# A sampling table with one column of two rows per entry, read two entries at a time

## The chip, the core and the metric

The kernel runs on one core of a Trainium2 chip. The core has a matrix engine (PE), a vector engine (DVE), a scalar engine (ACT), a general engine (POOL), a queue engine that only issues transfers (SP), and 16 DMA engines that all queues share. The metric is the time on the device in microseconds, as the median of several runs. Beside the timed runs there is one execution under the hardware profiler; its trace and its page of sums are what this document quotes.

## What is computed

The reference takes a batch of eight images of 64 channels and 128 x 128 pixels through four layers. The first is a deformable convolution, and only this layer is touched. For every pixel and each of the nine taps of a 3 x 3 kernel, two small convolutions give an offset and a mask; the image is sampled at the shifted place by bilinear interpolation, which needs four neighbouring pixels:

```
def corner(yi, xi, wgt):
    valid = (yi >= 0) & (yi < H) & (xi >= 0) & (xi < W)
    ...
    return vals * (wgt * valid)[None]
return corner(y0, x0, wy0 * wx0) + corner(y0, x0 + 1, wy0 * wx1) + corner(y0 + 1, x0, wy1 * wx0) + corner(y0 + 1, x0 + 1, wy1 * wx1)
...
sampled = sampled * mask[:, None]
return jnp.einsum('bckhw,ock->bohw', sampled, weight.reshape(O, C, KK))
```

The other layers are a 3 x 3 convolution, a bidirectional state-space scan over rows and columns, and a search for the nine least similar pixels of a window, followed by a convolution. Everything is in 32-bit floats. In the kernel the image is normalised before the deformable layer, in groups of two channels.

## The kernel before

The images are handled in four pairs. Two images of 64 channels fill the 128 partitions.

**The stages of the first layer.** `deform` (from L176) holds four generators. `statistics(p)` loads a pair in eight pieces and gathers mean and variance. `fill(p)` (L272 to L302) writes a sampling table in HBM for each of the two images. `offsets(p, e)` computes the offsets of eight image rows: it loads the rows into `xe` (L310), normalises them on ACT, and runs the offset convolutions as a long chain of matmuls (L322) for each group of four rows; results are transposed back (`to`) and `positions` (from L341) turns them into table indices `idx` and four weights per sample `wts` on DVE. `sample(p, g, ...)` (from L376) does the sampling proper for four image rows.

**The table.** One entry of the table stands for one pixel place and holds four pixels of 64 channels: the place itself, the one below, the one to the right, and that one's lower neighbour. That is 256 floats, or 1,024 bytes. The table has `CELL` = 131 rows and 131 columns of such entries, with borders of zeros for places outside the image. The zeros are written once, before anything else, by DMAs from ACT's queue (L201, L203, L204). Two pairs of tables are used in turn.

**The fill.** It runs in 33 steps. A step takes four image rows: PE transposes them (L289), so that a partition is a column of the image; DVE and ACT copy them into a tile `q` (L291 to L293) as two-row columns, where each column holds a pixel and the one below it, 128 floats. Then four DMAs go out on SP's queue: for each of the two images, the same `q` is written once into the left half of entries (L299) and once, one column further left, into the right half (L300). Image pieces `xt` of 16 rows are loaded on the same queue (L285), into two buffers; `q` has three buffers.

**The gather.** For every partition (one image column), image row and tap, one entry is fetched. POOL issues one indirect DMA for 128 samples (L388); nine of them fill a tile `g`, of which there are four. DVE multiplies a gathered entry by its four weights (L397) and adds the four products (L398) into `sm`; PE transposes `sm` (L402, L404), ACT copies it (L405, L406), and at the end of four rows PE applies the weights of the deformable convolution (L411). There are 4 pairs x 32 groups x 72 gathers = 9,216 gathers.

**The order.** The first table and the first offsets are made before any sampling: `run(statistics(0))`, `run(fill(0))`, `run(offsets(0, 0))`. After that the sampling loop advances the next offsets after every ninth gather, and the statistics and the fill of the next pair after every third of these. A scheduler lays out the instructions of each engine ahead of time, and the engines keep to that order. An indirect DMA waits for all writes to its table; so the first gather comes after the whole first fill.

Of the kernel before, what the change touches and what calls it, by code (L numbers as in the profile page):

```python
# [9 lines left out]
F32 = mybir.dt.float32  # L10
I32 = mybir.dt.int32
AF = mybir.ActivationFunctionType
ALU = mybir.AluOpType
# [3 lines left out]
P = 128  # L17
C = 64
H = 128
# [2 lines left out]
NCH = HW // CH  # L22
ROOM = 2 * (H // 2 + 1) * H
CELL = H + 3
QW = 4 * C
NS = 64
T = 4
NB = 256
# [12 lines left out]
class Net:  # L41
# [134 lines left out]
    def deform(self):  # L176
        tc, nc, ins = self.tc, self.nc, self.ins
# [5 lines left out]
        with ExitStack() as ctx:  # L183
# [6 lines left out]
            bias = cp.tile([54, 1], F32, name="bias")  # L190


            tables = [[self.dram.tile([CELL, CELL, QW], F32, name=f"table{s}{i}") for i in range(2)] for s in range(min(2, self.npair))]
            with tc.tile_pool(name="a_setup", bufs=1) as sp:
                zeros = sp.tile([P, 6 * C], F32, name="zeros")
                nc.gpsimd.memset(zeros, 0.0)
                for table in (t for pair in tables for t in pair):
                    flat = table.rearrange("a b q -> a (b q)")
                    n = CELL * QW // P
                    for row in (0, CELL - 1):  # L200
                        nc.scalar.dma_start(flat[row : row + 1, :].rearrange("a (p n) -> (a p) n", p=P), zeros[:, 0:n])  # L201
                    for r0, r1 in ((1, CELL - 1 - 1), (CELL - 2, CELL - 1)):
                        nc.scalar.dma_start(flat[r0:r1, 0 : 6 * C], zeros[0 : r1 - r0, :])  # L203
                        nc.scalar.dma_start(flat[r0:r1, CELL * QW - 6 * C :], zeros[0 : r1 - r0, :])  # L204
                whv = sp.tile([P, 2, 15, 2, 9], F32, name="whv")
                wmm = sp.tile([P, 9, 9], F32, name="wmm")
                for i in range(2):
                    rows = slice(i * C, (i + 1) * C)
                    nc.sync.dma_start(whv[rows, 0], ins["wh"])
                    nc.sync.dma_start(whv[rows, 1], ins["wv"])  # L210
                    nc.sync.dma_start(wmm[rows], ins["wm"])
                for i in range(2):
                    rows = slice(i * C, (i + 1) * C)
                    for d in range(-7, 8):
                        if d:
                            nc.vector.tensor_copy(wt[rows, at[0, d], 0:2, i, :], whv[rows, 0, d + 7])
                            nc.gpsimd.tensor_copy(wt[rows, at[d, 0], 0:2, i, :], whv[rows, 1, d + 7])
                    nc.vector.tensor_add(wt[rows, 0, 0:2, i, :], whv[rows, 0, 7], whv[rows, 1, 7])
                    for a in range(3):
                        for b in range(3):  # L220
                            nc.vector.tensor_copy(wt[rows, at[a - 1, b - 1], 2, i, :], wmm[rows, 3 * a + b])
                bh = sp.tile([36, 2], F32, name="bh")
                for d in range(2):
                    for i in range(2):
                        to = slice(18 * d + 9 * i, 18 * d + 9 * i + 9)
                        for n, b in enumerate(("bh", "bv")):
                            nc.sync.dma_start(bh[to, n : n + 1], ins[b][d].rearrange("(k o) -> k o", o=1))
                nc.vector.tensor_add(bias[0:36, :], bh[:, 0:1], bh[:, 1:2])
                for i in range(2):
                    nc.sync.dma_start(bias[36 + 9 * i : 45 + 9 * i, :], ins["bm"].rearrange("(k o) -> k o", o=1))  # L230
# [41 lines left out]
            def fill(p):  # L272

                r, nb = norms[p]
                table = tables[p % len(tables)]

                q = qp.tile([P, 2, 4, 2, C], F32, tag="q", name=f"q{p}_0")
                nc.gpsimd.memset(q[:, :, 0, 0, :], 0.0)
                for g in range(NCH + 1):
                    n = 4 if g < NCH else 1  # L280
                    if g < NCH:
                        if g % 4 == 0:
                            xs = xp.tile([P, 16, H], F32, tag="xs", name=f"xt{p}_{g}")
                            xf = xs.rearrange("p h w -> p (h w)")
                            nc.sync.dma_start(xf, self.x[p * P : (p + 1) * P, g * CH : (g + 4) * CH])  # L285
                            nc.scalar.activation(xf, xf, AF.Identity, bias=nb, scale=r)
                        tp = ps_t.tile([P, 4, 2, C], F32, tag="tp", name=f"tp{p}_{g}")
                        for m in range(4):
                            nc.tensor.transpose(tp[:, m].rearrange("p i c -> p (i c)"), xs[:, 4 * (g % 4) + m, :], self.ident)  # L289
                        nxt = qp.tile([P, 2, 4, 2, C], F32, tag="q", name=f"q{p}_{g + 1}")  # L290
                        nc.vector.tensor_copy(q[:, :, :, 1, :].rearrange("p i r c -> p r i c"), tp)  # L291
                        nc.scalar.copy(q[:, :, 1:4, 0, :].rearrange("p i r c -> p r i c"), tp[:, 0:3])
                        nc.vector.tensor_copy(nxt[:, :, 0, 0, :], tp[:, 3])  # L293
                    else:
                        nc.gpsimd.memset(q[:, :, 0, 1, :], 0.0)
                    for i in range(2):
                        rows = table[i][4 * g + 1 : 4 * g + 1 + n]
                        src = q[:, i, 0:n].rearrange("p r t c -> p r (t c)")
                        nc.sync.dma_start(rows[:, 2 : 2 + H, 0 : 2 * C].rearrange("r w e -> w r e"), src)  # L299
                        nc.sync.dma_start(rows[:, 1 : 1 + H, 2 * C :].rearrange("r w e -> w r e"), src)  # L300
                    q = nxt
                    yield  # L302

            def offsets(p, e):
# [8 lines left out]
                for g in (2 * e, 2 * e + 1):  # L313
# [22 lines left out]
                    nc.vector.tensor_copy(off[:, :, 4 * (g % 2) : 4 * (g % 2) + 4, :].rearrange("p d r n -> p r d n"), tp)  # L336
                    yield
                ready[p, e] = positions(p, e, off)
                yield

            def positions(p, e, off):  # L341

                n = 8 * 18
                h0 = 8 * e
                pos = op.tile([P, 2, n], F32, tag="pos", name=f"pos{p}_{e}")
                cell = op.tile([P, 2, n], F32, tag="cell", name=f"cell{p}_{e}")
                up = op.tile([P, 2, n], F32, tag="up", name=f"up{p}_{e}")
                o = off.rearrange("p d r n -> p d (r n)")
                nc.vector.scalar_tensor_tensor(pos[:, 0], base_y, float(h0), o[:, 0], ALU.add, ALU.add)
                nc.vector.tensor_add(pos[:, 1], base_x, o[:, 1])  # L350

                nc.vector.tensor_scalar(pos, pos, -2.0, float(H), ALU.max, ALU.min)
                whole = up.bitcast(I32)
                nc.vector.tensor_copy(whole, pos)
                nc.vector.tensor_copy(cell, whole)
                nc.vector.tensor_tensor(up, cell, pos, ALU.is_gt)
                nc.vector.tensor_sub(cell, cell, up)

                nc.vector.tensor_sub(pos, pos, cell)
                nc.vector.tensor_scalar(up, pos, -1.0, 1.0, ALU.mult, ALU.add)  # L360
                idx = wp.tile([P, n], I32, tag="idx", name=f"idx{p}_{e}")
                nc.vector.scalar_tensor_tensor(cell[:, 0], cell[:, 0], float(CELL), cell[:, 1], ALU.mult, ALU.add)
                nc.vector.tensor_scalar_add(idx, cell[:, 0], float(2 * CELL + 2))
                mask = o[:, 2]
                nc.scalar.activation(mask, mask, AF.Sigmoid)
                nc.vector.tensor_mul(pos[:, 0], pos[:, 0], mask)
                nc.vector.tensor_mul(up[:, 0], up[:, 0], mask)
                w = wtp.tile([P, n, 2, 2], F32, tag="wts", name=f"wts{p}_{e}")
                for b, wx in ((0, up), (1, pos)):
                    for a, wy in ((0, up), (1, pos)):  # L370
                        nc.vector.tensor_mul(w[:, :, b, a], wx[:, 1], wy[:, 0])
                w = w.rearrange("p n b a -> p n (b a)")
                wts = [w[:, 0 : n // 2], w[:, n // 2 :]]
                return idx, wts
# [47 lines left out]

            run(statistics(0))
            run(fill(0))
            run(offsets(0, 0))
            for p in range(self.npair):
# [4 lines left out]
                for e in range(NCH // 2):  # L431
# [12 lines left out]
                    idx, wts = ready.pop((p, e))  # L444
# [933 lines left out]
```

## Time and profile before

| what | us |
|---|---|
| median of three timed runs | 16,778.65 |
| lowest and highest of them | 16,744.45 and 16,786.79 |
| the profiled execution | 18,868.66 |
| its span, first to last instruction | 18,866.9 |
| first table write issued, first gather | 81.7 and 233.1 |
| last gather | 14,066.5 |

The profiled execution took some 12% longer than the timed runs, so sums made from its rows stand against its own time. A row of the page's fifth part reads: line, engine, operation, what is written and read, how many; then busy time in total and the mean of one in ns; then the engine's idle time just before and what ended it. A line of a stage gives start and end, the length, busy time and count for PE, PE's weight loads, DVE, ACT and POOL, the granted clock of PE as a share, the mean busy share of the 16 DMA engines and GB/s. Issuing a DMA is not counted as busy time, except on POOL[...].

The transfers of the page, in packets, megabytes and share of the engines' time:

```profile
q0 software_dynamic: 442368, 1208.55, 21.9%
q1 hardware_dynamic: 519524, 751.65, 13.1%
```

The first is the queue of the gathers (9,216 x 128 x 1,024 bytes), the second SP's queue, with the table writes among its traffic.

### The profile page before, as it was taken

The numbers are of one execution on the slowest core, as the hardware profiler recorded it, in microseconds if no ns is written. First come the engines' busy times: TensorE is split into PE (matmuls) and PEld (weight loads), VectorE is DVE, ScalarE is ACT, GpSimd is POOL, SyncE is SP. The second block draws the span as 40 slices with busy tenths as digits, with TensorE's granted clock in tenths as the row PEclk, the third lists the DMA queues.
The fourth block names the chain that finished last, engine by engine and source line by source line (L and its number), as shares of the span: only waits on it lengthen the run. The fifth ranks groups of instructions, "written<-read, shape, count | busy, mean of one in ns | idle before, by whom it ended". The sixth has DMA issues, their size and how long they took to land. (4 is left out here: it accounts for less than half of the span.)

```text
span 18866.9 us, 120155 instructions
## 1 busy us (share of the span) xinstructions
PE 11118.0 (59%) x31864; PEld 4087.3 (22%) x31864; DVE 11443.6 (61%) x27208; ACT 2993.5 (16%) x5596; POOL 11190.9 (59%) x10484
## 2 busy tenths in 40 slices
PE   4654445545555444545544554455328988888886
PEld 1111111111111111111111111111104444444443
DVE  4565666665665556656656565556564755657566
ACT  1000010010100000111000000000013424334242
POOL 3676777677666677676767767667762414324142
PEclk7776776767777666777777776667659989989898
DMA  5333344334433333444333333333332242432423
GB/s 177 97 102 97 120 132 124 115 123 125 127 118 97 95 98 112 122 129 125 101 92 98 97 96 100 95 95 98 90 119 63 65 143 77 118 91 75 133 75 97
DMA packets 1036955, 2006.36 MB, mean 106 GB/s; under 512 B 204140, under 2 KB 572148, under 8 KB 1012724
## 3 DMA queue, kind: packets, MB, share of 16 engines
q0 software_dynamic: 442368, 1208.55, 21.9%
q1 hardware_dynamic: 519524, 751.65, 13.1%
q10 hardware_dynamic: 74384, 38.46, 0.9%
q8 instruction: 260, 4.26, 0.1%
q14 instruction: 419, 3.43, 0.1%
HBM read 1544.92 MB, written 276.80 MB: 97 GB/s over the span
## 5 line engine op out<-in xcount | busy, mean ns | idle before, releaser
L388 POOL DMA_INDIRECT g<-table,idx x9216 | 9704.6, 1053 | 4132.2 <-issue 2620.7
L398 DVE TENSOR_REDUCE sm<-g 128x64 f32<-128x256 f32 x9216 | 5039.8, 580 | 2991.7 <-remote 2020.0
L322 PE MATMUL po<-xe,wt 128*54 128x512 f32 (+3 forms) x8384 | 4637.8, 663 | 295.7 <-ACT ob L332 177.5
L402 PE MATMUL sp<-ident,sm 128*128 128x128 f32 x4096 | 1499.5, 376 | 4621.1 <-DVE sm L398 2058.2
L397 DVE TENSOR_TENSOR g<-g,wts 128x256 f32<-128x256 f32 x9216 | 3538.2, 415 | 663.8 <-DMA g<-table,idx 577.6
L402 PEld LDWEIGHTS sp<-ident,sm 128*128 128x128 f32 x4096 | 620.7, 155 | 7332.1 <-DVE sm L398 2490.0
L405 ACT COPY s<-sp 128x512 f32<-128x512 f32 x1024 | 598.9, 585 | 9839.8 <-PE sp L402 4174.9
L411 PE MATMUL yp<-s,wd 128*64 128x512 f32 (+1 forms) x2560 | 875.3, 700 | 925.6 <-ACT s L405 560.9
L322 PEld LDWEIGHTS po<-xe,wt 128*54 128x54 f32 x8384 | 913.8, 138 | 1618.9 <-issue 1156.8
L412 DVE BATCH_NORM_STATS2 ystat<-yp 128x6 f32<-128x512 f32 x128 | 89.2, 697 | 1318.5 <-remote 838.5
L839 POOL COPY l_yb<-ln_y 128x512 f32<-128x512 f32 x128 | 79.0, 658 | 1309.6 <-PE l1v L833 1166.7
L562 PE MATMUL c<-room,l_w 128*64 128x508 f32 (+1 forms) x3072 | 741.6, 597 | 21.7 <-DMA room<-nx 15.5
L1205 POOL TENSOR_TENSOR u<-u,v 128x512 f32<-128x512 f32 x256 | 330.9, 1292 | 696.0 <-DVE v L1204 515.2
L1297 POOL TENSOR_TENSOR ms<-ms,ln_y 128x512 f32<-128x512 f32 x256 | 278.3, 1107 | 743.6 <-DVE ln_y L118 711.5
L404 PE MATMUL s<-ident,sm 128*64 128x128 f32 x1024 | 344.6, 337 | 628.4 <-DVE sm L398 267.1
L1187 ACT ACTIVATE fx<-room,ln_b,ln_g 128x512 f32<-128x512 f32 x512 | 639.4, 1294 | 118.7 <-DMA in<-fx 99.6
L1220 DVE TENSOR_TENSOR_SCAN z<-tabs,z,u 128x256 f32<-128x256 f32 x512 | 445.2, 902 | 207.8 <-POOL u L1205 192.7
L1198 PE MATMUL pv<-in,tabs 128*128 128x512 f32 x1024 | 537.2, 649 | 45.9 <-DVE u L1204 45.9
L411 PEld LDWEIGHTS yp<-s,wd 128*64 128x64 f32 (+1 forms) x2560 | 229.9, 155 | 1378.5 <-issue 705.6
L1267 PE MATMUL py<-in,outs 128*128 128x512 f32 x1024 | 506.8, 608 | 2.2 <-ACT h L1269 1.5
L1267 PE MATMUL py<-x,outs 128*128 128x512 f32 x1024 | 502.4, 594 | 6.0 <-POOL x L1252 5.3
L1284 PE MATMUL pc<-outs,h 128*128 128x256 f32 x2048 | 498.1, 393 | 8.9 <-DVE h L1270 7.1
(406 smaller groups left out, 10444.8 us busy)
## 6 DMA issues: line engine op xcount, KB each, us to landing
g<-table,idx POOLq DMA_INDIRECT x9216
table<-q SPq DMA_DIRECT2D x512, 256.0 KB
in<-fx SPq DMA_DIRECT2D x1024, 128.0 KB
xe<-in_x_dram SPq DMA_DIRECT2D x56, 1408.0 KB
xs<-in_x_dram SPq DMA_DIRECT2D x32, 1024.0 KB
xt<-in_x_dram SPq DMA_DIRECT2D x32, 1024.0 KB
y<-ys SPq DMA_DIRECT2D x128, 256.0 KB
room<-in_x_dram SPq DMA_DIRECT2D x64, 512.0 KB
```

Source lines behind the costliest of these rows:

```text
L322: nc.tensor.matmul(po[:, r0:r1, c0:c1], lhsT=wt[:, t, :], rhs=xe[:, row + r0 : row + r1, c0 + dx : c1 + dx], start=n == 0, stop=n == len(u ...
L388: nc.gpsimd.indirect_dma_start(out=tq[:, k, :], out_offset=None, in_=flat[i], in_offset=bass.IndirectOffsetOnAxis(ap=idx[:, at : at + 1], ...
L397: nc.vector.tensor_mul(t[:, k], t[:, k], w)
L398: nc.vector.tensor_reduce(sm[:, k], t[:, k].rearrange("p q c -> p c q"), axis=mybir.AxisListType.X, op=ALU.add)
L402: nc.tensor.transpose(sp[:, j, :], sm[:, j * P : (j + 1) * P], self.ident)
L405: nc.scalar.copy(st[i][:, 0:4, m * P : (m + 1) * P], sp)
L411: nc.tensor.matmul(yp[i * C : (i + 1) * C, :], lhsT=wd[0:rows, j, :], rhs=st[i][0:rows, j, :], start=j == 0, stop=j == 4)
L562: nc.tensor.matmul(o, lhsT=lt, rhs=mv, start=k < 2, stop=k >= len(calls) - 2)
L1187: nc.scalar.activation(fx[:, e].rearrange("p h (o m) -> p h o m", m=self.INNER), src[:, e::2], AF.Identity, bias=w["ln1_b"], scale=w["ln1_g"])
L1198: nc.tensor.matmul(pv, lhsT=tabs[:, at : at + P], rhs=fx[:, :, h, :], start=h == 0, stop=h == 1)
L1267: nc.tensor.matmul(py, lhsT=lt, rhs=mv, start=n == 0, stop=n == len(calls) - 1)
L1284: nc.tensor.matmul(pc[:, i], lhsT=hs[:, h, i, m * P : (m + 1) * P], rhs=self.outs[:, CEN : MIX + P], start=True, stop=True)
```

## The change

An entry of the table is now one column of two rows: a pixel and the one below it, 128 floats or 512 bytes. A row of the table has `LINE` = 132 entries instead of 131. Since the right-hand half of a sample is the left-hand half of the next place, the fill writes each column once, and a gather reads 256 floats from the start of its entry, which are two entries in a row. The index is multiplied by `LINE` instead of `CELL`, and the zero borders shrink with the table. The two gathered halves stand in the same order as before, so that weights, products and sums are unchanged. Each pixel now stands in the table twice, once as the upper and once as the lower pixel of a column; before, it stood there four times.

```diff
 CELL = H + 3
-QW = 4 * C
+LINE = H + 4
+PW = 2 * C
...
-            tables = [[self.dram.tile([CELL, CELL, QW], F32, name=f"table{s}{i}") for i in range(2)] for s in range(min(2, self.npair))]
+            tables = [[self.dram.tile([CELL, LINE, PW], F32, name=f"table{s}{i}") for i in range(2)] for s in range(min(2, self.npair))]
             with tc.tile_pool(name="a_setup", bufs=1) as sp:
-                zeros = sp.tile([P, 6 * C], F32, name="zeros")
+                zeros = sp.tile([P, 2 * PW], F32, name="zeros")
...
-                    n = CELL * QW // P
+                    n = LINE * PW // P
...
-                        nc.scalar.dma_start(flat[r0:r1, 0 : 6 * C], zeros[0 : r1 - r0, :])
-                        nc.scalar.dma_start(flat[r0:r1, CELL * QW - 6 * C :], zeros[0 : r1 - r0, :])
+                        nc.scalar.dma_start(flat[r0:r1, 0 : 2 * PW], zeros[0 : r1 - r0, :])
+                        nc.scalar.dma_start(flat[r0:r1, (LINE - 2) * PW :], zeros[0 : r1 - r0, :])
...
                         src = q[:, i, 0:n].rearrange("p r t c -> p r (t c)")
-                        nc.sync.dma_start(rows[:, 2 : 2 + H, 0 : 2 * C].rearrange("r w e -> w r e"), src)
-                        nc.sync.dma_start(rows[:, 1 : 1 + H, 2 * C :].rearrange("r w e -> w r e"), src)
+                        nc.sync.dma_start(rows[:, 2 : 2 + H, :].rearrange("r w e -> w r e"), src)
...
-                nc.vector.scalar_tensor_tensor(cell[:, 0], cell[:, 0], float(CELL), cell[:, 1], ALU.mult, ALU.add)
-                nc.vector.tensor_scalar_add(idx, cell[:, 0], float(2 * CELL + 2))
+                nc.vector.scalar_tensor_tensor(cell[:, 0], cell[:, 0], float(LINE), cell[:, 1], ALU.mult, ALU.add)
+                nc.vector.tensor_scalar_add(idx, cell[:, 0], float(2 * LINE + 2))
```

The gather itself keeps its text; only the row length of `flat` behind it changes from 256 to 128 floats:

```
nc.gpsimd.indirect_dma_start(
    out=tq[:, k, :],
    out_offset=None,
    in_=flat[i],
    in_offset=bass.IndirectOffsetOnAxis(ap=idx[:, at : at + 1], axis=0),
)
```

Line numbers here and below are those of the kernel before.

## The prediction

> **What bounds the kernel now.** I read the page's engine sums first, then the stages one by one, then the rows of the line that gathers, then the queues.
>
> Busy time over the whole span names no bound: three engines lie near 60%.
>
> ```profile
> PE 11118.0 (59%) x31864; PEld 4087.3 (22%) x31864; DVE 11443.6 (61%) x27208; ACT 2993.5 (16%) x5596; POOL 11190.9 (59%) x10484
> ```
>
> So the span is cut into stages (microseconds from the start; busy time per engine, granted clock, share of the 16 DMA engines, GB/s). The first line is the filling of the first table, the next three lie in the sampling of the four pairs, the last is all that follows.
>
> ```profile
> 81.00:233.00 152.00, 88.58 (x268) 37.10 (x269) 34.23 (x84) 35.46 (x45) 0.41 (x2) 0.73 0.90 275
> ...
> 2196.00:3482.00 1286.00, 675.85 (x1672) 195.85 (x1672) 797.86 (x1924) 137.73 (x266) 912.79 (x866) 0.72 0.42 127
> ...
> 5500.00:7606.00 2106.00, 1031.66 (x2465) 288.73 (x2464) 1255.21 (x3003) 176.45 (x365) 1457.91 (x1394) 0.70 0.33 100
> ...
> 14070.00:18866.00 4796.00, 3996.28 (x14727) 2074.14 (x14727) 2908.00 (x6517) 1707.13 (x3003) 1471.95 (x1204) 0.91 0.34 96
> ```
>
> From 81 to 233 us the DMA engines are at 0.90 and every engine is far below. The DMA view of that stretch (40 slices of 3.8 us) shows how full they are: 284 to 287 GB/s wherever tables are written, and three holes where the next images are waited for.
>
> ```profile
> DMA  5999999997099999999996999999996299999997
> GB/s 159 284 287 285 286 284 291 287 339 286 9 279 285 284 286 287 286 285 279 410 433 199 286 285 286 285 285 284 287 362 255 71 284 284 284 287 287 287 285 213
> ...
> table<-q SPq DMA_DIRECT2D x128, 256.0 KB
> xt<-in_x_dram SPq DMA_DIRECT2D x6, 1024.0 KB
> xe<-in_x_dram SPq DMA_DIRECT2D x1, 1408.0 KB
> ```
>
> In sampling the DMA engines stand at a third, and POOL carries the time: 9,216 gathers in 13,837 us (233 to 14,070), 1.50 us each. The rows of the gather and of its two readers on DVE, then the view of the table's users:
>
> ```profile
> L388 POOL DMA_INDIRECT g<-table,idx x9216 | 9704.6, 1053 | 4132.2 <-issue 2620.7
> L398 DVE TENSOR_REDUCE sm<-g 128x64 f32<-128x256 f32 x9216 | 5039.8, 580 | 2991.7 <-remote 2020.0
> ...
> L397 DVE TENSOR_TENSOR g<-g,wts 128x256 f32<-128x256 f32 x9216 | 3538.2, 415 | 663.8 <-DMA g<-table,idx 577.6
> ...
> L388 POOL DMA_INDIRECT g<-table,idx x9216: 940/946/2370, 233.1 to 14066.5; - x197
> ...
>   issue: 2620.7, 8587
>   DVE sm L398: 1137.0, 342
> ...
>   DMA table<-q: 4.7, 1
> ```
>
> The reader is to see that a gather costs POOL 1.05 us and 0.3 us of issue, that only 1.1 ms of its idle time waits for DVE, and that it waited for a table write once: 4.7 us, before the first gather.
>
> **What the Trainium skill says.** The "Perfetto Trace Analysis" page (DMA Instruction — SWDGE (GPSIMD)) says that the profiled window of such a DMA is the writing of its descriptors, not the movement. The trace agrees: the q0 row of the page, the gathers' own packets, fills 21.9% of the engines while POOL is at its limit. "DMA: Bandwidth & Descriptors" (How a descriptor splits into AXI transactions) says that a run starting on a multiple of 256 bytes is cut into 256-byte transactions with nothing extra fetched. By that a gather starting on a multiple of 512 costs the same four transactions as one on a multiple of 1,024; all gathers before start on multiples of 1,024, so no run here shows it yet. "SBUF — State Buffer" (Who interferes with whom) says that a DVE instruction with two SBUF inputs holds off a GpSimd instruction that reads SBUF. The trace fits: the median gather is 946 ns and the mean 1,053, as if a quarter of them ((1053 - 946) / 415 = 0.26) sat out one 415 ns product of L397.
>
> **The change part by part.**
>
> *The gather.* The count stays 9,216, and each still fetches 128 runs of 1,024 bytes; the built instruction differs only in the step that the index is multiplied by, 512 bytes for 1,024. POOL's instructions stand in the same order in both programs. Nearest row: L388 itself, 1,053 ns. Bounds per gather: below, -1% (-10 ns), since the table is half as large and neighbours share bytes; above, 946 ns more, if each run became two of 512 bytes. I take 0, as the instruction says 1,024 bytes. This is the number on which everything hangs: 1 ns per gather is 9.2 us.
>
> *Table writes in the first fill.* Before, each of 33 steps issues four DMAs, after, two (the last step's are 64 KB). Removed from the stretch: 64 x 256 KB and 2 x 64 KB = 16.9 MB. At 286 GB/s: 59 us. Nothing lay over it, for the DMA engines were full and the first gather waits for the whole table.
>
> What is late next: (a) DMA again: 16.9 MB of writes at 286 GB/s (59 us) and 7.7 MB of loads at about 400 GB/s (19 us; the slices with loads read 410 and 433) make 78 us. (b) PE: in its timeline the matmuls of L322 for the first offsets add up to 53 us between 81 and 144 us, and 32 groups of four transposes at 0.66 to 1.1 us are 21 to 35 us: 74 to 88 us, in order. (c) SP: 66 issues of at most 0.88 us, 58 us. (d) ACT 35 us and DVE 34 us busy. So PE and DMA end nearly together, at 81 + 78 to 95 us. The new order helps the loads: SP issues an image after six table writes, before after 32, which is where the holes come from. But it mixes the L322 matmuls among the transposes all the way, so that writes can wait behind matmuls, and the transposes of the offsets come last, with some 9 us of position arithmetic on DVE after them. I expect the first gather at 165 to 185 us, for 233: a gain of 48 to 68 us. I take 57, close to the removed bytes.
>
> *Zeros.* The borders shrink from 2.6 to 1.6 MB. SP stands 9.3 us in front of L826 for `table<-zeros`, and the statistics' loads are behind it. Gain between 0 and 5 us; I take 1.
>
> *Fills of pairs 1 to 3.* 198 writes fewer. They lie beside gathers, and the stage lines tell what they cost: with writes 1286 us / 866 gathers = 1.485 us each, without them 2106 / 1393 = 1.512 us. No price is visible; bounds -20 to +20 us; I take 0. On SP the xe loads and y stores get ahead earlier, but POOL has no wait for them.
>
> *Index arithmetic* (L362, L363): other constants, same instructions: nothing.
>
> *Sum* against the profiled execution: 18,866.9 us of span (18,868.7 measured around it) less 58. The timed runs have a median of 16,778.65 us, 2,090 less; this difference is not in the fill, which the DMA engines set, so I carry the 58 us over unscaled: 16,720 us.
>
> **The rivals.**
>
> B, *PE or the loads take over*. The start gains only 30 to 50 us: the fill's transposes queue behind matmuls and the DMA engines fall idle. For it: the PE sum of 74 to 88 us beside 78 us of DMA. Against it: PE was idle for 63 of the 152 us before. Time: 16,729 to 16,749.
>
> C, *the sampling shifts too*. If landings come at other moments, another share of gathers meets a product on DVE: one point of share is 0.01 x 9,216 x 415 ns = 38 us. For it: POOL and DVE run in step, and half the table is half as much memory to touch. Against it: 1.485 and 1.512 us with different traffic beside. A gain of two points: about 16,640.
>
> D, *slower: a gather off the 1,024-byte grid costs more.* Place: L388, all four pairs. Half of the runs now cross a 1,024-byte boundary, and if the descriptor work or the landing grows by that, POOL's bound grows. At 6 ns per gather the gain is gone (58 / 9.2), at 12 ns the kernel is slower by over 0.3%. Price for 20 ns: +184 us, 16,905. If the runs were really cut in two, up to 9,216 x 0.946 us = 8.7 ms. For it: nothing in the page, only that no gather of this kind was seen. Against it: the instruction's 1,024 bytes, and DMA engines at a third: 22% x 18,867 us / 9,216 = 0.45 us per gather of 1.50, so the movement could treble unseen.
>
> That the change doesn't do what it says: the write list and the instruction's step show that it does; no chance is set aside.
>
> **How the numbers follow.** A, the forecast, 0.60; B 0.18; C 0.12; D 0.10. About 0.3% (50 us) can be told from no change here. A lies just past this mark, and I give 0.50 of its 0.60 to faster and 0.10 to the same; C is faster, B the same, D slower. Faster 0.62, same 0.28, slower 0.10. A alone spans 16,690 to 16,750 (48 to 68 us, and the 20 us by which runs differ). The range reaches down to C's 16,640 and up past B to 16,790; the larger part of D is left out.
>
> **What would show it.** Right: the first gather starts at 165 to 185 us; 264 table writes instead of 528 and queue q1 about 68 MB smaller; L388 at 940 to 946 ns median and a mean within 10 ns of 1,053; 1.49 to 1.51 us per gather. Wrong in size: ACT or PE idle in the fill with the DMA share well below 0.9 (B). Wrong in kind: q0 with more than 442,368 packets, or a higher median of L388 (D), or a mean that moves at the same median (C).

## The result and the profile after

The changed kernel takes 16,687.07 us (median of 5 runs, 16,671.60 to 16,690.23), before 16,776.03 us (16,744.45 to 16,786.79): 89 us less, a ratio of 0.9949 with an interval of 0.9935 to 0.9964. Measured twice more beside fresh runs of before it gave 0.9951 (0.9938 to 0.9965; 16,684.38 for 16,755.60 us) and 0.9951 (0.9937 to 0.9964; 16,692.71 for 16,776.90 us). The gain is 71 to 89 us.

The execution of before that the prediction was read from took 18.87 ms, while all timed runs beside the changed kernel lie near 16.77 ms, so before is read here from a second profiled execution (the first experiment), with a span of 16,778.5 us.

The page of the changed kernel, lines that answer to those of before: busy sums, the two queues, the rows of the gather and its readers on DVE (busy, mean ns, idle before). A line of a view has the number of the kernel that the view is of: L389, L398 and L399 here are L388, L397 and L398 of before.

```profile
PE 11226.6 (67%) x31864; PEld 4101.4 (25%) x31864; DVE 11600.4 (70%) x27208; ACT 2990.4 (18%) x5596; POOL 10394.8 (62%) x10484
...
q0 software_dynamic: 442368, 1208.55, 24.4%
q1 hardware_dynamic: 383204, 684.00, 13.4%
...
L389 POOL DMA_INDIRECT g<-table,idx x9216 | 8908.4, 967 | 2809.5 <-issue 2613.6
L398 DVE TENSOR_TENSOR g<-g,wts 128x256 f32<-128x256 f32 x9216 | 3818.1, 420 | 3101.9 <-DMA g<-table,idx 3084.0
L399 DVE TENSOR_REDUCE sm<-g 128x64 f32<-128x256 f32 x9216 | 4988.3, 580 | 0.8 <-DVE pos L353 0.2
```

The gathers' queue carries the same packets and bytes: the runs are still 1,024 bytes. SP's queue is 67.65 MB smaller (751.65 before). POOL waits for almost nothing but its own issue, and DVE waits for landings. So it is in the second trace of before, too:

```profile
L388 POOL DMA_INDIRECT g<-table,idx x9216 | 8925.5, 968 | 2811.3 <-issue 2615.5
L397 DVE TENSOR_TENSOR g<-g,wts 128x256 f32<-128x256 f32 x9216 | 3805.2, 420 | 3130.2 <-DMA g<-table,idx 3112.9
```

The view of the table's users in the changed kernel gives median and place of the gathers (ns least/median/most, then start of the first and of the last in us), the table writes, and what waited for them (us, times):

```profile
L389 POOL DMA_INDIRECT g<-table,idx x9216: 942/946/2878, 167.9 to 11883.7; - x197
L301 SPq DMA_DIRECT2D table<-q x264: 332/499/3023, 80.7 to 7568.8; - x132
...
  DVE q L295: 46.9, 18
```

The same view of before, second profiled execution:

```profile
L388 POOL DMA_INDIRECT g<-table,idx x9216: 942/946/2372, 233.3 to 11966.7; - x197
```

Two numbers come out of these lines. The first gather starts 65.4 us earlier (233.3 - 167.9). From first to last gather before needs 11,733.4 us and the changed kernel 11,715.8: 17.6 us less. What follows the last gather differs by 10 us here (4,811.8 and 4,801.3 us), but among the traces with a span below 17 ms it lies anywhere between 4,780 and 4,812 us, without a pattern.

In the first fill (stages as before: length, busy time per engine, granted clock, DMA share, GB/s; then 40 slices of 2.2 us) the changed kernel reads:

```profile
80.00:168.00 88.00, 77.60 (x257) 29.45 (x257) 32.00 (x77) 33.47 (x42) 0.56 (x3) 0.92 0.96 282
```

```profile
DMA  3999999999959999999997899999999999996891
GB/s 77 289 284 258 290 332 345 258 289 335 339 149 283 285 282 254 339 362 387 341 342 177 268 268 346 301 289 289 268 273 322 329 310 343 299 345 178 241 274 39
```

The mean rate is 282 GB/s for 275 before, the holes are gone (the DMA engines are idle for 0.04 of the stretch instead of 0.10), and PE is now busy for 78 of the 88 us. SP issues an image after six table writes, before after 32. Transfers still set the pace of the fill: the copies of L295 waited 46.9 us until table writes had read `q` (last line of the view above).

### The profile page after: what moved, and what is told of

Same layout as the page of the kernel before. It is cut to its first block, busy times and chain, and to the rows that moved or that the text cites. A ratio compares the mean times of both kernels' runs of the same rounds, so it can differ in the third digit from the quotient of the medians.

```text
span 16685.0 us, 119663 instructions
## 1 busy us (share of the span) xinstructions
PE 11226.6 (67%) x31864; PEld 4101.4 (25%) x31864; DVE 11600.4 (70%) x27208; ACT 2990.4 (18%) x5596; POOL 10394.8 (62%) x10484
## 5 line engine op out<-in xcount | busy, mean ns | idle before, releaser
L389 POOL DMA_INDIRECT g<-table,idx x9216 | 8908.4, 967 | 2809.5 <-issue 2613.6
L398 DVE TENSOR_TENSOR g<-g,wts 128x256 f32<-128x256 f32 x9216 | 3818.1, 420 | 3101.9 <-DMA g<-table,idx 3084.0
L399 DVE TENSOR_REDUCE sm<-g 128x64 f32<-128x256 f32 x9216 | 4988.3, 580 | 0.8 <-DVE pos L353 0.2
L323 PE MATMUL po<-xe,wt 128*54 128x512 f32 (+3 forms) x8384 | 4734.9, 676 | 44.4 <-ACT ob L333 42.5
L412 PE MATMUL yp<-s,wd 128*64 128x512 f32 (+1 forms) x2560 | 808.1, 652 | 12.6 <-ACT s L406 12.6
L1253 POOL TENSOR_TENSOR x<-x,xt 128x512 f32<-128x512 f32 x256 | 350.6, 1370 | 126.3 <-DVE xt L1252 126.0
L1285 PEld LDWEIGHTS pc<-outs,h 128*128 128x128 f32 x2048 | 382.5, 195 | 168.7 <-issue 65.4
```

Of the source, the lines that this page charges most:

```text
L323: nc.tensor.matmul(po[:, r0:r1, c0:c1], lhsT=wt[:, t, :], rhs=xe[:, row + r0 : row + r1, c0 + dx : c1 + dx], start=n == 0, stop=n == len(u ...
L389: nc.gpsimd.indirect_dma_start(out=tq[:, k, :], out_offset=None, in_=flat[i], in_offset=bass.IndirectOffsetOnAxis(ap=idx[:, at : at + 1], ...
L398: nc.vector.tensor_mul(t[:, k], t[:, k], w)
L399: nc.vector.tensor_reduce(sm[:, k], t[:, k].rearrange("p q c -> p c q"), axis=mybir.AxisListType.X, op=ALU.add)
L412: nc.tensor.matmul(yp[i * C : (i + 1) * C, :], lhsT=wd[0:rows, j, :], rhs=st[i][0:rows, j, :], start=j == 0, stop=j == 4)
L1285: nc.tensor.matmul(pc[:, i], lhsT=hs[:, h, i, m * P : (m + 1) * P], rhs=self.outs[:, CEN : MIX + P], start=True, stop=True)
```

## The experiments

The theories. W: the removed table writes are all of the gain, in the first fill and in the later ones. G: a part comes from the gather itself, which reads a smaller table from other places. S: the start is all. P: PE takes over the first fill, as in rival B. K: what the later fills cost in sampling is their copies on DVE, not their writes.

**Before once more.** No edit.

> The kernel before, unchanged, for a second profiled execution. The first one has a span of 18,867 us, 2,090 us over its timed runs, with 216 us per 144 gathers. If that surplus belongs to that one execution, the span here is within 1% of 16,776 us, the mean gather near 970 ns for 1,053, and a block of 144 gathers takes about 182 us without table writes and 186 to 187 us where the next table is written (after: 185). If it belongs to the kernel, the span is again near 18,870 us.

Measured: span 16,778.5 us, mean gather 968 ns. The surplus belongs to the first profiled execution, not to the kernel. Counted from the trace, a block of 144 gathers (eight image rows) takes 185.6 to 185.9 us where the next table is filled (means of the three fills) and 181.7 to 182.2 us without a fill (means of pairs 1 to 3), so a fill has a price, which the first trace did not show.

**First fill written twice.** The changed kernel, with the removed writes back in the first fill alone; they go to a spare pair of tables that nobody reads.

```diff
                         nc.sync.dma_start(rows[:, 2 : 2 + H, :].rearrange("r w e -> w r e"), src)
+                        if p == 0:
+                            more = spare[i][4 * g + 1 : 4 * g + 1 + n]
+                            nc.sync.dma_start(more[:, 2 : 2 + H, :].rearrange("r w e -> w r e"), src)
```

> The changed kernel, which writes in the first fill alone a second copy of each column into a spare table that nobody reads. Theory W (the writes are all of the gain: 65 us from the first fill, the rest of the 89 us from the fills of pairs 1 to 3): +55 to +70 us on the changed kernel, so 16,742 to 16,757 us; first gather at 225 to 235 us. Theory G (the gather from the smaller table gives a part of it, the first fill less): under +50 us. Theory P (PE bounds the first fill now): under +40 us.

Measured: 16,743.04 us beside 16,760.18 for before, a ratio of 0.9987 (0.9979 to 0.9996), as W expected. The view of the table's users and the DMA view of the first fill (40 slices of 3.8 us) of this kernel:

```profile
L393 POOL DMA_INDIRECT g<-table,idx x9216: 942/946/2371, 231.9 to 11947.9; - x197
```

```profile
DMA  3999999999089999999996999999997299999997
GB/s 103 285 287 286 286 284 289 289 318 369 15 248 285 285 286 285 285 286 281 397 437 219 283 287 286 287 284 286 285 358 283 64 285 285 285 284 288 287 286 227
```

The start of before is back with its holes: first gather 64.0 us later than in the changed kernel. From first to last gather it takes 11,716.0 us, as the changed kernel does (11,715.8). So the start's 65 us come from the removed writes, and the 17 us by which this kernel still beats before lie after the first gather. With the writes the order of the loads comes back, too: 32 writes lie between two images again. What the bytes save and what the order saves was not separated.

**Later fills written twice.** The same edit with `if p > 0`.

> The changed kernel with the second copy of each column written into a spare table in the fills of pairs 1 to 3 alone. Theory W: these writes are the other 24 us, so +15 to +30 us on the changed kernel, 16,702 to 16,717 us, seen as 186 to 187 us per 144 gathers in those stretches for 185. Theory G: 0 (within 8 us), as the gather is left as it is.

Measured: 16,687.40 us, a ratio to before of 0.9957 (0.9943 to 0.9970), 73 us under before. W's forecast of 16,702 to 16,717 us was missed: by its time this kernel can't be told from the changed one, which is 71 to 89 us under before. Its trace does differ:

```profile
L393 POOL DMA_INDIRECT g<-table,idx x9216: 942/946/2378, 167.3 to 11907.1; - x197
```

First to last gather is 11,739.8 us, 24 us more than in the changed kernel, and the blocks with a fill take 186.1 to 186.4 us (185.0 to 185.8 in the changed kernel). In the five traces with 198 later writes first to last lies between 11,715.8 and 11,721.9 us, in the three with 396 between 11,728.0 and 11,739.8. What follows the last gather is 17 us shorter in this trace than in that of the changed kernel, and hides the difference. So W holds for the start by time and by trace, for the later fills by the traces alone; S does not explain the traces. Nor does G: the gathers here read the small table and take as long as in before.

**The gather off the grid.** The kernel before, table shifted by 512 bytes, index in steps of 512 (the lines that shift the table are left out here).

```diff
-                nc.vector.tensor_scalar_add(idx, cell[:, 0], float(2 * CELL + 2))
+                nc.vector.tensor_scalar(idx, cell[:, 0], 2.0, float(2 * (2 * CELL + 2) + 1), ALU.mult, ALU.add)
...
-                flat = [table[i].rearrange("a b q -> (a b) q") for i in range(2)]
+                flat = [table[i].rearrange("(n q) -> n q", q=2 * C) for i in range(2)]
```

> The kernel before with its table of four pixels per entry shifted by 512 bytes: every gather starts at 512 past a multiple of 1,024, and its index counts steps of 512 bytes, as in the changed kernel. Table size and writes as before. Theory W: no difference from before (within 10 us), 16,766 to 16,786 us. Theory G in the form that the start of a gather matters: 16,750 us if it helps by the missing 24 us, over 16,790 us if it costs. Median gather 946 ns in any case.

Measured: 16,768.91 us beside 16,760.18, a ratio of 1.0006 (0.9998 to 1.0014).

```profile
L394 POOL DMA_INDIRECT g<-table,idx x9216: 942/946/2375, 233.7 to 11961.7; - x197
```

The start of a run and the step of the index have no price that can be seen. The Trainium skill, "DMA: Bandwidth & Descriptors" (How a descriptor splits into AXI transactions), says that a run which starts on a multiple of 256 bytes is split into transactions of 256 bytes, with no bytes fetched ahead of its start. The trace agrees: 946 ns, as on the grid. The table's smaller size by itself is not tested here; the kernel before this one has it.

**The changed kernel again**, as reference for the next three.

> The changed kernel itself, for a second measurement beside the same runs of before. The clean profile of before gives a sampling stage of 11,734 us (first gather 233.3, last block's end 11,967.7), the changed kernel 11,717 (167.9 to 11,884.7). Theory W: 65 us at the start and some 15 to 20 us in the fills of pairs 1 to 3, so 75 to 95 us under before, ratio 0.9943 to 0.9955. If the fills of pairs 1 to 3 gain nothing (theory S, the start alone): 60 to 70 us, ratio 0.9958 to 0.9964.

Measured: 16,684.38 us for 16,755.60, 0.9951; first gather at 166.8 us, first to last 11,719.6 us. The 71 us lie between what S (60 to 70) and W (75 to 95) expected; the split is carried by the traces and by the first fill written twice, not by this total.

**No later writes.** The fills of pairs 1 to 3 write nothing, and all pairs sample the first table.

```diff
-                    for i in range(2):
+                    for i in range(2 if p == 0 else 0):
...
-                        sample(p, 2 * e + half, tables[p % len(tables)], idx, wts[half], work)
+                        sample(p, 2 * e + half, tables[0], idx, wts[half], work)
```

> The changed kernel without the table writes of pairs 1 to 3: their fills still load, normalise, transpose and copy, but write nothing, and all pairs sample the first pair's table, so that three quarters of the deformable layer's samples are of other images. Theory W: the blocks of 144 gathers in those stretches fall from 185.4 us towards 182 us by half the price or more, in all -20 to -60 us on the changed kernel. Rival K (the copies on DVE make the price, not the writes): the blocks stay at 185 us and the time within 10 us.

Measured: 16,664.85 us, 20 us less, at the edge of what W expected.

```profile
L389 POOL DMA_INDIRECT g<-table,idx x9216: 942/946/2370, 168.1 to 11865.8; - x197
```

First to last 11,697.7 us, and blocks with a fill at 183.7 to 183.8 us. So the second half of the writes costs about what the first did. Three quarters of the samples are here of other images, all from one pair of tables; that this alone moves the gathers is not excluded.

**Copies on ACT.** The two copies of each later fill step that DVE made go to ACT.

```diff
-                        nc.vector.tensor_copy(q[:, :, :, 1, :].rearrange("p i r c -> p r i c"), tp)
+                        copy = nc.vector.tensor_copy if p == 0 else nc.scalar.copy
+                        copy(q[:, :, :, 1, :].rearrange("p i r c -> p r i c"), tp)
...
-                        nc.vector.tensor_copy(nxt[:, :, 0, 0, :], tp[:, 3])
+                        copy(nxt[:, :, 0, 0, :], tp[:, 3])
```

> The changed kernel with the two DVE copies of each fill step of pairs 1 to 3 on ACT, which is about 12% busy in sampling; writes unchanged. Rival K: the blocks with a fill fall from 185.4 to about 182 us, -50 to -70 us. Theory W: they stay at 185 us, within 15 us of the changed kernel.

Measured: 16,650.85 us, 34 us less than the changed kernel; blocks with a fill at 183.3 to 184.1 us.

```profile
L390 POOL DMA_INDIRECT g<-table,idx x9216: 942/946/1642, 169.0 to 11852.8; - x197
```

More than W allowed and less than K wanted: both carry a part, 34 us for the place of 192 copies and about 20 us for 198 writes. The longest gather falls from 2,878 to 1,642 ns.

How the writes reach POOL can be counted in the traces. Most gathers take 946 ns. Those of 1,000 ns and more, and among them those that begin while DVE runs a product of a gathered tile:

| kernel | later writes | gathers of 1,000 ns or more | begun during a product | their time over 946 ns, us | first to last gather, us |
|---|---|---|---|---|---|
| before | 396 | 816 | 771 | 205.8 | 11,733.4 |
| later fills twice | 396 | 843 | 793 | 212.6 | 11,739.8 |
| changed | 198 | 714 | 673 | 189.9 | 11,715.8 |
| no later writes | 0 | 662 | 612 | 171.3 | 11,697.7 |
| copies on ACT | 198 | 689 | 642 | 156.6 | 11,683.8 |

The fifth column (all gathers of the third) accounts for the last: -15.9 of -17.6 us from before to changed, -18.6 of -18.1 without later writes, -33.3 of -32.0 with the copies on ACT. So the writes don't hold the gather's queue; more gathers last long. What these meet shows at the moment when they begin: in the changed kernel 673 of the 714 begin during a product (L397 of before, 420 ns), but only 435 of the 8,502 shorter ones. (A product or a reduction lies beside 97% of the shorter ones, too, so that alone tells nothing.) Of the gathers under 1,500 ns that begin during a product, the median takes 946 ns where under 120 ns of the product are left, and 141, 203 and 249 ns more where 240 to 300, 300 to 360 and 360 to 420 ns are left. That is not the whole account: with 180 to 240 ns left it takes 281 ns more, and with over 420 ns left none. The long gathers that begin during a product carry the whole saving: their time over 946 ns is 196.8 us on average in the three traces with 396 later writes and 181.9 us in the five with 198, 15 us less, as it is from first to last gather.

The Trainium skill, "SBUF — State Buffer" (Who interferes with whom), says that a DVE instruction with two SBUF inputs contends with a GpSimd instruction that reads SBUF; the products are such instructions, and the gather reads its indices from SBUF. The same section infers that a TENSOR_TENSOR, which such a product is, does not stall the writing of descriptors; for these gathers the count decides against that. Why the writes move gathers onto products is not shown: the median landing is 2.7 to 2.8 us with and without them.

The copies act in another way. Only 6 of the 714 long gathers begin during a copy of a fill. But 16 gathers of the changed kernel take over 2,000 ns, all of them while a table is filled. They begin during a product, DVE goes on with the arithmetic of `positions` (L361 to L372 of this kernel), and they end just after it (start and length in us):

```profile
2715.98 0.41 DVE L398 TENSOR_TENSOR g<-g,wts 128x256 f32<-128x256 f32 x1
2716.32 0.30 DVE L361 TENSOR_SCALAR up<-pos 128x288 f32<-128x288 f32 x1
2716.32 2.37 POOL L389 DMA_INDIRECT g<-table,idx  x1 [0.30 <-issue]
...
2718.09 0.42 DVE L372 TENSOR_TENSOR wts<-pos 128x144 f32<-128x144 f32 x1
```

These 16 carry 24.5 us over 946 ns. With the copies on ACT no gather takes over 2,000 ns, which is most of the 33.3 us. How the copies bring the arithmetic to that moment stays open.

**Images kept.** Five of the first pair's eight image pieces stay in SBUF from the statistics (the lines that keep them are left out here).

```diff
-                            xs = xp.tile([P, 16, H], F32, tag="xs", name=f"xt{p}_{g}")
...
+                            if p == 0 and g > 8:
+                                xf = kept[g // 4]
+                                xs = xf.rearrange("p (h w) -> p h w", w=H)
```

> The changed kernel with the last five of the first pair's eight image pieces kept in SBUF from the statistics, so that the first fill doesn't load them again: 5 MB less in a stretch of 88 us whose DMA engines are at 0.96 with 282 GB/s. If the transfers still set the end of the first fill: -14 to -19 us, first gather at 149 to 154 us. If PE does (77.6 of 88 us busy): at most -10 us, first gather at 158 us or later.

Measured: 16,661.58 us, 23 us less than the changed kernel, of which the trace shows 11 at the start (first gather 155.6 for 166.8) and none in the gathers (11,721.9 us from first to last). Its table writes in the first fill, its DMA view from 80 to 168 us (2.2 us a slice) and PE's timeline before the first gather:

```profile
L306 SPq DMA_DIRECT2D table<-q x66: 359/533/1487, 64.7 to 131.8; - x66
...
DMA  9749998899997999899978593000111059544454
```

```profile
137.56 9.35 PE L328 MATMUL po<-xe,wt 128*54 128x496 f32 x22
149.23 0.45 PE L341 MATMUL to<-ident,ob 54*128 54x54 f32 x4 [2.32 <-ACT ob L338]
149.62 10.87 PE L328 MATMUL po<-xe,wt 128*54 128x512 f32 x21
```

The DMA engines are done with the fill at about 134 us; then come the rest of the offset matmuls, their transposes and the positions on DVE, for which POOL's first gather waits. Neither forecast was right as put: the first gather lies between 154 and 158 us. Nor is 11 us the price of 5 MB: the edit also moves the fill forward, and its first table write goes out at 64.7 us (80.3 in the changed kernel), while small loads that stood ahead of it come after. What can be said is that with less to load the offset matmuls on PE set the end.

**Both edits together**, measured first on a chip on which before takes 18,829 us:

> The changed kernel with both edits that gained alone: the fills' copies of pairs 1 to 3 on ACT (-34 us) and five image pieces of the first pair kept in SBUF (-23 us timed, -11 us by the first gather). They touch different stretches, so they should add: -45 to -57 us on the changed kernel, 16,627 to 16,640 us, ratio to before 0.991 to 0.993; first gather at 155 us, 183 us per 144 gathers in the fills.

There it took 18,810.92 us beside 18,828.51 for before, a ratio of 0.9994 (0.9983 to 1.0005): no gain that can be told, though its first gather starts at 153.6 us. The view of the table's users shows what is different on that chip: the waits of POOL for DVE.

```profile
L395 POOL DMA_INDIRECT g<-table,idx x9216: 940/946/1774, 153.6 to 13982.2; - x197
...
  DVE sm L405: 1161.5, 346
```

In the second trace of before this wait is 138.0 us, in the first it is 1,137.0. The two have more in common: 13,828.6 us from first to last gather here and 13,833.4 in the first trace of before, mean granted PE clocks of 0.762 and 0.760 (0.817 in the second). Why DVE stands so long there stays open, and so does what the changed kernel alone gains there. The changed kernel and this one were then measured beside before once more:

> The changed kernel once more, as the reference of the next one. On a chip where before takes about 16,760 us: 75 to 90 us less than before. On a chip where before takes about 18,830 us (one such showed DVE waiting long in sampling, 216 us per 144 gathers): 65 us of the start remain if only that stretch differs, so a ratio near 0.9965; nearer 1.000 if the sampling there swallows or hides the gain.

Measured: 16,692.71 us for 16,776.90, 84 us less.

> The changed kernel with the later fills' copies on ACT and five image pieces kept, again, beside it. On a chip at 16,760 us for before: 45 to 57 us less than the changed kernel, ratio to before 0.991 to 0.993. On a chip at 18,830 us: within 25 us of the changed kernel, as there 17 us against before were all that remained.

Measured: 16,651.47 us, 41 us under the changed kernel, a little less than the 45 to 57 forecast, and 125 under before, a ratio of 0.9920 (0.9907 to 0.9934). The two edits nearly add, and this version beats both kernels.

## Why the prediction was right

*The gather* was priced at 0, and no cost can be seen: same packets, same median, and off the grid the same again. Rival D falls with it.

*The first fill* was put at 57 us and gave 65. The removed bytes over 286 GB/s (59 us) account for most of it. The rest fits the holes, which the new order of loads closed, and which I had named but not counted; no run separates the two.

*PE as the next limit*, rival B, did not bite, but was near: PE was busy for 78 of 88 us, while the fill's copies still waited 46.9 us for table writes. Of SP's issues I read 0.88 us as the most; the view has 0.916 us, which makes 60 us of the 58.

*Zeros*: 1 us taken, and the first table write starts 1.0 to 2.2 us earlier (80.7 for 81.7 and 82.9).

*The fills of pairs 1 to 3* are the term that was mis-sized. I took 0, "no price is visible", from 1.485 us per gather with writes and 1.512 without. Those stages came from an execution in which POOL waited 1,137.0 us for DVE's reductions (138.0 in the second trace) and 2,800 gathers took 1,000 ns or more (816). The second trace shows a price, and the runs put what the change saves at 15 to 18 us: first to last gather is 11,733.7 us on average with 396 later writes (three traces) and 11,718.7 with 198 (five). With the 65 us of the start that makes about 80 us instead of 58, amid the three measurements of 71 to 89; the forecast's own span of 16,690 to 16,750 us is reached only by the slowest of the three medians (16,684, 16,687 and 16,693 us). The mechanism is the one that rival C named, gathers meeting products on DVE: 98 fewer begin during one, of 9,216. That is one point of share instead of two, and it is worth 15 to 18 us instead of the 38 that C reckoned for a point.

*The carry-over* of the 58 us from an execution of 18.87 ms held for the fill, which the DMA engines set there too (first gather at 233.1 and 233.3 us), but not for the rows of L388: the forecast of a mean of 1,053 ns and 1.50 us per gather was wrong for every later trace with a span below 17 ms (963 to 969 ns, 1.27 us), for before as for after. In this there was luck: where before takes 18,829 us, even both further edits together left no gain that can be told, and the timed runs of the change were not made there.

## What to carry to other kernels

Before a stage is read for small prices, compare the profiled execution's span with the timed runs: where they differ by a tenth, stages set by transfers may still carry over, but a mean row over a contested engine does not. A write that lies beside other work is not free when the engine it delays indirectly is the bound: here 198 hidden writes cost 15 to 20 us, in gathers that meet a product on DVE. And what such a gather meets is seen from what runs when it begins, not from what lies beside it. And a gather may start at any entry and run on into the next, so overlapping samples need not be stored twice.

## What was not expected of the hardware

On one chip before takes 18,829 us and on others 16,756 to 16,779; the difference lies in sampling, where a block of 144 gathers takes 216 us for 182 to 186. And the copies of the later fills on DVE cost the gathers 34 us, though hardly a long gather begins during one: 24.5 us of it are in 16 gathers that wait out the arithmetic of the positions.
